# A four-layer graph network on one core: which source tiles of layer 3 are multiplied already during layer 2

## The chip, the core and the metric

The kernel runs on one core of one Trainium2 chip. The metric is the device time of one execution in microseconds, smaller being better; three runs of the kernel before have a median of 3042.52 us (3040.0 to 3048.64). A separate execution was profiled; the profile rows come from that one. The engines are named as in the profile: PE multiplies matrices (PEld is its weight load), DVE works on vectors, ACT on activations and copies, POOL issues the gathers, SP and the ACT queue issue the plain transfers.

## The reference

A graph has 6250 nodes with 256 features each and 100,000 edges, sorted by destination; destinations crowd at low node numbers (a uniform number squared). The features are layer-normed and clipped at zero, and four graph layers and a final product follow:

```python
h = sage_mean(h)   # h @ W1_self + mean over in-edges of h[src] @ W1_neigh + b1
h = sage_pool(h)   # h @ W2_self + max over in-edges of relu(h @ W2_pool + b)[src] @ W2_neigh + b2
h = sage_gcn(h)    # (sum over in-edges of h[src] + h) / (deg + 1) @ W3_neigh + b3
h = sage_mean(h)   # as layer 1, with W4
out = x + (h @ W_fc + b_fc)
```

The weights of layers 3, 4 and the last product are multiplied together ahead of time, so layer 3 sums rows of 512 numbers and layer 4 rows of 256.

## The kernel before

**Tiles.** Nodes stand in 49 tiles of 128 rows (`NT`), edges in 782 columns of 128 (`T`). A destination tile with a low number has very many edges. For those the kernel does not gather row by row: it makes a *count matrix* (how often does each source node appear among the edges of this destination), one 128 x 128 block for each pair of destination and source tile, and multiplies it with the source rows. `HUB = (8, 16, 18)` says for how many destination tiles that is done in layers 1, 3 and 4. In layer 3 these are the destinations 0 to 15, and each needs all 49 source tiles. The remaining destinations of a layer come out of `sums`: one indirect gather of 128 rows for each edge column, and three products with a one-hot matrix that add them up (rows are kept as three bf16 parts, hence three products).

**Layer 2** takes a maximum[...], so all 782 edge columns are gathered by POOL (`X<-tab_p,srcIf`, L1144), compared along runs of equal destinations by DVE (L1149), and written back by SP (`runb<-X`, L1190). The counter `at` numbers these columns: "step" below always means this counter. The columns are walked in six blocks from the last to the first, of 100, 130, 180, 220, 100 and 52 steps, so blocks end at steps 100, 230, 410, 630, 730 and 782. In the last three blocks two neighbouring columns are merged before they are written, which is one more DVE operation for every two steps (L1185). When a block is finished, a carry is passed between its 128 rows (`carry`), and then the destination tiles whose edges begin in it can be finished: `done2(d)` gathers the maxima (`tot`, L1053), transposes them, multiplies with the weights (`pm_prf`, L1077, L1080, L1083), and writes the row of tile `d` in three parts (`r`, L286 to L289) to `tab_r` (L1093). Tiles are finished from 48 down to 0; a new one is started about every 13 steps from step 112, or later where its block is not done.

**Work put beside the steps.** Behind each step a fixed portion of other work is written into the program:

- `hub.advance` makes the count matrices of destinations 8 to 15 until step `EARLY_AT` = 250, then those of 16 and 17 (destinations 0 to 7 were made in layer 1). They go to `tab_a`.
- `early.advance` does layer 3's products that are possible already. When four finished tiles (`BATCH`) of the range `EARLY` are there, `early_products` adds, for each of the 16 destinations, one load of four count blocks (`ae<-tab_a`, L1115, 64 KB, on SP's queue), 12 products (`pd<-r,ae`, L442), and one addition to the destination's sum (`acc`, `add3`: the first on ACT at L944, the others on DVE at L941). Below, these 12 products with their load and their addition are called a *parcel*; there are 8 x 16 = 128 of them. At each step a fortieth of what waits is done.

A row tile `r` stands in a ring of 9 buffers; it becomes free when the last product that reads it is done. The generators only write the program; a planner of the framework then sets the order on each engine, so the order in the built program need not be the order in which the generators ran.

**Layer 3** begins when `tab_r` is complete. The 17 source tiles outside `EARLY` are loaded as three resident pieces (`zt<-tab_r`, L1240), and the products of 16 destinations with them are spread over the gathered columns (`ring<-tab_r`, L386, and `pg`, L404). A gathered destination 16 to 48 also adds its own row: from the resident piece if it lies there (`d in Z3`), else by a load of 384 KB (`zown<-tab_r`, L1264) three steps ahead; `pm_own` (L1270) is the product that brings it in. The result goes to `tab_s`, and layer 4 begins after the last of it.

Of the kernel before, what the change touches and what calls it, by code (L numbers as in the profile page):

```python
# [10 lines left out]
BF16 = mybir.dt.bfloat16  # L11
# [9 lines left out]
P = 128  # L21
# [7 lines left out]
Z_SIGMA = 5.0  # L29
WIN = 8  # L30
HUB = (8, 16, 18)
EARLY = (6, 38)
MADE_AT = 64
FIRST_AT = 112
EARLY_AT = 250
# [43 lines left out]
def fast_path(  # L79
# [18 lines left out]
    FH = W1_self.shape[1]  # L98
    FO = W_fc.shape[1]
    NT = (N + P - 1) // P  # L100
# [37 lines left out]
    H1, H3, H4 = HUB  # L138
# [82 lines left out]
    at = 0  # L221
# [9 lines left out]
    def bank(pool, tag, name, shape=None, bufs=None):  # L231
        t = pool.tile([P, FH], F32, tag=tag, name=name, **({"bufs": bufs} if bufs else {}))
        if shape is None:
            return t
        n = math.prod(shape)
        if len(shape) == 1:
            return t[:, :n]
        return t[:, :n].rearrange("p (a b) -> p a b", b=shape[1])
# [566 lines left out]
    with ExitStack() as on:  # L805
# [10 lines left out]
        def done1(d, acc):  # L816
# [23 lines left out]
            for k in range(KI):  # L840
# [12 lines left out]
                        lambda acc, d=d: todo.append(done1(d, acc)), extra=1)  # L853
                  for d in range(H1)]
        work = list(builds[0])
# [90 lines left out]
    with tc.tile_pool(name="fl2c", bufs=1) as ck, ExitStack() as late:  # L946
# [102 lines left out]
        def totals(d):  # L1049
            tots = []  # L1050
            for b in range(b_of[d][0], b_of[d][1] + 1):
                t = wk.tile([P, FH], F32, name="tot", bufs=4)
                nc.gpsimd.indirect_dma_start(  # L1053
                    out=t, out_offset=None, in_=runs[b],
                    in_offset=bass.IndirectOffsetOnAxis(ap=rows_of[b][:, d : d + 1], axis=0),
                )
                tots.append(t)
            th = wk.tile([P, 2 * KI, P], F32, name="th2", bufs=2)
            nc.scalar.dma_start(th, tab_t[d].rearrange("p (k n) -> p k n", n=P))
            return tots, th  # L1060

        def done2(d):
            tots, th = totals(d)
            for _ in range(4):
                yield
            hm = tots[0]
            for t in tots[1:]:
                nc.vector.tensor_tensor(hm, hm, t, op=ALU.max)
            yield
            pt = bank(pst, "pt", "pt_hTf", (KH, P))  # L1070
            for j in range(KH):
                nc.tensor.transpose(pt[:, j, :], hm[:, j * P : (j + 1) * P], ident)
            hT = wk.tile([P, KH, P], F32, name="hTf")
            nc.scalar.copy(hT, pt)  # L1074
            pm = bank(psm, "pm", "pm_prf")
            for k in range(KI):
                nc.tensor.matmul(pm, th[:, k, :], usA[:, k, :], start=(k == 0), stop=False)  # L1077
            yield
            for k in range(KI):
                nc.tensor.matmul(pm, th[:, KI + k, :], usB[:, k, :], start=False, stop=False)  # L1080
            yield
            for c in range(KH):
                nc.tensor.matmul(pm, hT[:, c, :], un[:, c, :], start=False, stop=(c == KH - 1))  # L1083
                if c == 1:
                    yield
            pr = wk.tile([P, FH], F32, name="prf")
            nc.vector.tensor_add(pr, pm, prow)
            yield
            if d < H3:
                add3(d, pr)  # L1090
            r3 = early_pool[0].tile([P, 3 * FH], BF16, name="r3", bufs=2 * BATCH + 1)
            parts(pr, FH, r3)
            nc.sync.dma_start(tab_r[d * P : (d + 1) * P, :], r3)  # L1093
            if EARLY[0] <= d < EARLY[1]:
                ready.append((d, r3))
                if len(ready) == BATCH or d == EARLY[0]:
                    early_products()
            yield


        BATCH = 4
        ready = []
        early = Hub()
        early_pool = []

        def early_products():
            batch = dict(ready)
            ss = sorted(batch)
            ready.clear()
            for d in range(H3):  # L1110
                got = {}

                def load(d=d, got=got):
                    got[0] = early_pool[0].tile([P, BATCH, P], F8, name="ae", bufs=LOOK + 3)
                    nc.sync.dma_start(got[0][:, : len(ss), :].bitcast(BF16),  # L1115
                                      tab_a[d, :, ss[0] : ss[-1] + 1, :])

                work = dense(ss, lambda s, got=got: got[0][:, s - ss[0], :],
                             lambda s: batch[s], FH, psd, lambda v, d=d: add3(d, v))
                early.add([(load, work[0])] + work[1:])  # L1120


        todo = [chains(), node_rows(wk, psm)]
# [10 lines left out]
        at = 0  # L1134
        for b in reversed(range(NB)):
            tb = BLOCKS[b]
            t0 = offs[b] // P
            prev = None
            for s0 in range(0, tb, G2):
                n = min(G2, tb - s0)  # L1140
                X = (xmore if at // G2 % 2 else xpool).tile([P, G2, FH], F32, name="X2")
                for k in range(n):
                    t = t0 + s0 + k
                    nc.gpsimd.indirect_dma_start(  # L1144
                        out=X[:, k, :], out_offset=None, in_=tab_p,
                        in_offset=bass.IndirectOffsetOnAxis(ap=srcI[:, t : t + 1], axis=0),
                    )
                    if s0 + k:
                        nc.vector.scalar_tensor_tensor(  # L1149
                            X[:, k, :], prev, same[:, t : t + 1], X[:, k, :],  # L1150
                            op0=ALU.mult, op1=ALU.max,
                        )
                    prev = X[:, k, :]
                    at += 1
                    if at > 8:
                        next(steps, None)
                        if todo and next(todo[0], 0) == 0:
                            todo.pop(0)
                    if at == MADE_AT:
                        for _ in steps:  # L1160
                            pass
                        top.close()
                        early_pool.append(
                            top.enter_context(tc.tile_pool(name="early3", bufs=1)))
                    if at <= EARLY_AT:
                        hub.advance(math.ceil(len(first) * max(0, at - 16) / (EARLY_AT - 16)))
                    else:
                        hub.advance(len(first) + math.ceil(
                            len(rest) * (at - EARLY_AT) / (T - 100 - EARLY_AT)))
                    early.advance(early.done + math.ceil(early.left() / 40))  # L1170
                    if s0 + k > 2 and ends and next(ends[0], 0) == 0:
                        ends.pop(0)
                        tiles += [d for d in reversed(range(NT)) if b_of[d][0] == last_b]
                    if tiles and not ends and begun2 < NT * (at - FIRST_AT) / (T - 20 - FIRST_AT):
                        now.append(done2(tiles.pop(0)))
                        begun2 += 1
                    for g in list(now):
                        if next(g, 0) == 0:
                            now.remove(g)
                r0 = s0  # L1180
                if b < MERGED:
                    r0 = s0 // 2
                    if s0 + n < tb:
                        t = t0 + s0 + 1
                        nc.vector.scalar_tensor_tensor(  # L1185
                            X[:, 0, :], prev, same[:, t : t + 1], X[:, 0, :],
                            op0=ALU.mult, op1=ALU.max,
                        )
                        n = 1
                nc.sync.dma_start(  # L1190
                    runs[b][r0 * P : (r0 + n) * P, :].rearrange("(g p) f -> p g f", p=P),
                    X[:, :n, :],
                )
            end = carry(b, prev)
            next(end)
            ends.append(end)
            last_b = b
# [45 lines left out]
    with ExitStack() as on:  # L1243
# [8 lines left out]
        with tc.tile_pool(name="fl3", bufs=2) as wk:  # L1252
# [29 lines left out]
                    if d == s1 - 1:  # L1282
                        Z4.update(resident(zk, tab_s, FO, s0, s1))

            late = ((EARLY[1], 44), (44, NT), (0, EARLY[0]))
            Z3 = {}
            for s0, s1 in late:
                Z3.update(resident(wk, tab_r, FH, s0, s1))
# [2 lines left out]
            work = []  # L1291
            for d in range(H3):
                work += dense([s for s0, s1 in late for s in range(s0, s1)], lambda s, d=d: block(d, s), lambda s: Z3[s], FH, psd,
                              lambda acc, d=d: todo.append(done3(d, acc)))
# [3 lines left out]
        with tc.tile_pool(name="fl4", bufs=2) as wk:  # L1298
# [19 lines left out]
            work = []  # L1318
            for d in range(H4):
                work += dense([s for s0, s1 in order for s in range(s0, s1)],  # L1320
                              lambda s, d=d: block(d, s), lambda s: Z4[s], FO, psd,
                              lambda acc, d=d: todo.append(done4(d, acc)))
# [644 lines left out]
```

## Time and profile before

| what | value |
|---|---|
| median of three runs | 3042.52 us |
| the profiled execution: its time, its span | 3044.61 us, 3042.8 us |
| PE busy | 2459.1 us (81%) |
| DVE busy | 2039.5 us (67%) |
| POOL busy | 2051.3 us (67%) |
| mean granted PE clock | 0.909 |
| layer 2, first gather to last write of `tab_r` | about 824 to 2148 us |
| layer 3, from there to layer 4's first load | about 2148 to 2622 us |

The span is what lies between the first and the last instruction; 1.8 us of the execution lie around it. A busy share is an average over stages with different limits, so it says little by itself; what matters is which engine is full in which stage. "Releaser" or "waited for" names what ended an idle time.

### The profile page before, as it was taken

How to read it: one execution, taken by the hardware profiler on the slowest of the kernel's cores; microseconds unless marked ns; L12 is line 12 of the kernel's file. 1: busy time of each engine (PE TensorE's matmuls, PEld its weight loads, DVE VectorE, ACT ScalarE, POOL GpSimd, SP SyncE). 2: the span in 40 equal slices, each digit the busy share in tenths (PEclk: the TensorE clock that was granted, in tenths of full speed). 3: DMA queues.
4: the chain of work that ended last, by engine and by line, in shares of the span. 5: the costliest groups of instructions: out<-in, count | busy, mean ns of one | idle time of the engine just before them, and what ended most of it. 6: DMA issues, size and time to landing. Idle time of an engine off the chain costs nothing. (4 is left out here: it accounts for less than half of the span.)

```text
span 3042.8 us, 41553 instructions
## 1 busy us (share of the span) xinstructions
PE 2459.1 (81%) x12699; PEld 1402.3 (46%) x12699; DVE 2039.5 (67%) x5161; ACT 905.7 (30%) x2383; POOL 2051.3 (67%) x2260
## 2 busy tenths in 40 slices
PE   1468999999778664767789994983699999799999
PEld 0234666666543321323334442431234444488888
DVE  4956767766378788666779997987266676444433
ACT  2557766765255666421111110100000001000000
POOL 5274777776366676777767777765477777677775
PEclk9787999999999776788899997996799999899999
DMA  6454667776599999999989998987799999878886
GB/s 191 148 158 134 202 206 213 213 214 206 165 387 354 334 390 376 363 387 387 371 275 318 323 315 280 310 287 223 291 368 385 383 381 375 310 234 239 247 239 193
DMA packets 380021, 865.41 MB, mean 284 GB/s; under 512 B 58078, under 2 KB 151238, under 8 KB 379756
## 3 DMA queue, kind: packets, MB, share of 16 engines
q0 software_dynamic: 146560, 514.74, 51.8%
q1 hardware_dynamic: 175144, 292.49, 25.9%
q10 hardware_dynamic: 58084, 55.44, 5.8%
q8 instruction: 103, 1.69, 0.2%
q14 instruction: 130, 1.06, 0.1%
HBM read 610.65 MB, written 252.60 MB: 284 GB/s over the span
## 5 line engine op out<-in xcount | busy, mean ns | idle before, releaser
L1144 POOL DMA_INDIRECT X<-tab_p,srcIf x782 | 839.8, 1074 | 384.5 <-issue 161.5
L404 PE MATMUL pg<-ring,hot 128*128 128x256 bf16 (+2 forms) x3390 | 682.6, 310 | 78.3 <-DMA ring<-tab_h,srcT 34.8
L442 PE MATMUL pd<-zt,ac 128*128 128x256 bf16 (+1 forms) x3462 | 566.8, 299 | 21.6 <-DMA ac<-tab_a 12.2
L386 POOL DMA_INDIRECT ring<-tab_h,srcT x474 | 451.5, 952 | 195.8 <-PE pg L404 76.9
L404 PEld LDWEIGHTS <-hot 128*128 128x128 bf16 x3390 | 332.7, 99 | 303.1 <-issue 134.9
L442 PE MATMUL pd<-r,ae 128*128 128x512 bf16 x1536 | 378.5, 396 | 96.5 <-DVE acc L941 45.2
L386 POOL DMA_INDIRECT ring<-tab_r,srcE x342 | 330.6, 967 | 146.5 <-PE pg L404 63.6
L442 PEld LDWEIGHTS <-ac 128*128 128x128 fp8e4 x3462 | 339.4, 98 | 151.7 <-issue 21.0
L311 ACT ACTIVATE hs<-ht,onef 128x128 bf16<-128x128 bf16 x781 | 292.3, 395 | 305.3 <-PE pb L319 303.6
L319 PE MATMUL pb<-hm,hs 128*128 128x392 bf16 x781 | 257.4, 380 | 152.4 <-ACT A L324 109.4
L386 POOL DMA_INDIRECT ring<-tab_s,srcE x314 | 298.7, 951 | 112.8 <-issue 60.5
L423 DVE SCALAR_TENSOR_TENSOR acc<-pg,M,acc 128x257 f32<-128x257 f32 (+2 forms) x518 | 273.0, 561 | 151.4 <-PE pg L404 150.6
L1149 DVE SCALAR_TENSOR_TENSOR X<-X,samef 128x512 f32<-128x512 f32 x391 | 292.0, 748 | 97.6 <-DMA X<-tab_p,srcIf 84.0
L1149 DVE SCALAR_TENSOR_TENSOR X<-X,samef,X 128x512 f32<-128x512 f32 x385 | 287.2, 747 | 92.9 <-DMA X<-tab_p,srcIf 46.1
L442 PEld LDWEIGHTS <-ae 128*128 128x128 fp8e4 x1536 | 155.1, 101 | 330.4 <-issue 153.2
L382 DVE TENSOR_SCALAR hot<-iota_bf,keyE 128x128 bf16<-128x128 bf16 x656 | 153.5, 268 | 132.2 <-PE pg L404 126.0
L1083 PE MATMUL pm_prf<-unf,hTf 128*128 128x512 f32 x392 | 199.6, 637 | 2.8 <-ACT hTf L1074 2.8
L319 PEld LDWEIGHTS <-hs 128*128 128x128 bf16 x781 | 81.9, 105 | 249.5 <-issue 165.3
L442 PE MATMUL pd<-Z,A 128*128 128x256 bf16 (+1 forms) x1176 | 189.1, 274 | 0.3 <-ACT A L324 0.2
L313 DVE TENSOR_SCALAR hm<-iota_w,mk 128x392 bf16<-128x392 f16 x461 | 154.5, 344 | 46.0 <-PE pb L319 44.8
L324 ACT ACTIVATE A<-pb 128x392 fp8e4<-128x392 f32 x288 | 139.3, 486 | 147.7 <-DVE most L323 113.8
L323 DVE TENSOR_REDUCE most<-pb 128x1 f32<-128x392 f32 x288 | 160.8, 559 | 32.6 <-PE pb L319 31.9
(288 smaller groups left out, 2881.9 us busy)
## 6 DMA issues: line engine op xcount, KB each, us to landing
runb<-X SPq DMA_DIRECT2D x208, 512.0 KB
runb<-X SPq DMA_DIRECT2D x183, 256.0 KB
tab_r<-r SPq DMA_DIRECT2D x49, 384.0 KB
tab_a<-A SPq DMA_DIRECT2D x18, 784.0 KB
tab_t<-th SPq DMA_DIRECT2D x49, 256.0 KB
tab_p<-hpf SPq DMA_DIRECT2D x49, 256.0 KB
th<-tab_t ACTq DMA_DIRECT2D x49, 256.0 KB
X<-tab_p,srcIf POOLq DMA_INDIRECT x782
```

The lines of the kernel that those rows point to most:

```text
L311: nc.scalar.activation(hots[0], t, AF.Relu, bias=one, scale=-1.0)
L313: nc.vector.tensor_scalar(hots[1], iota_w, mk[:, r : r + 1], None, op0=ALU.is_equal)
L319: nc.tensor.matmul(hold[0], hots[0], hots[1], start=(k == 0), stop=(k == k_of[w] - 1))
L323: nc.vector.tensor_reduce(most[:, w : w + 1], hold[0], AX.X, ALU.max)
L382: nc.vector.tensor_scalar(hot[j], iota_b, keyT[:, j - jb : j - jb + 1], None, op0=ALU.is_equal)
L386: nc.gpsimd.indirect_dma_start(out=ring[:, j % deep, : 3 * F], out_offset=None, in_=table, in_offset=bass.IndirectOffsetOnAxis(ap=srcT[:, ...
L404: nc.tensor.matmul(pg[:, : F + c], hot[j], X[:, part * F : (part + 1) * F + c], start=(k == 0 and part == 2), stop=(k == n - 1 and part == 1),
L423: nc.vector.scalar_tensor_tensor(acc[d], pg, m, acc[d], op0=ALU.mult, op1=ALU.add)
L442: nc.tensor.matmul(hold[0][:, : F + c], a, z[:, part * F : (part + 1) * F + c], start=(s == ss[0] and part == 2), stop=(s == ss[-1] and pa ...
L1083: nc.tensor.matmul(pm, hT[:, c, :], un[:, c, :], start=False, stop=(c == KH - 1))
L1144: nc.gpsimd.indirect_dma_start(out=X[:, k, :], out_offset=None, in_=tab_p, in_offset=bass.IndirectOffsetOnAxis(ap=srcI[:, t : t + 1], axis=0),
L1149: nc.vector.scalar_tensor_tensor(X[:, k, :], prev, same[:, t : t + 1], X[:, k, :], op0=ALU.mult, op1=ALU.max,)
```

## The change

`EARLY` becomes 17 to 48: layer 2 multiplies the tiles that are finished first, and the residents of layer 3 are the tiles 0 to 16 that are finished last. The first two batches are then ready before the count matrices of destinations 8 to 15 exist; their parcels are collected in `later` and added at step 257. The ring of row tiles grows from 9 to 16. In `done2`, eight steps instead of four lie between the gather of the maxima and their use.

```diff
-EARLY = (6, 38)
+EARLY = (17, 49)
@@ done2
             tots, th = totals(d)
-            for _ in range(4):
+            for _ in range(8):
                 yield
@@
-            r3 = early_pool[0].tile([P, 3 * FH], BF16, name="r3", bufs=2 * BATCH + 1)
+            r3 = early_pool[0].tile([P, 3 * FH], BF16, name="r3", bufs=4 * BATCH)
@@
         early = Hub()
+        later = []
@@ early_products
-                early.add([(load, work[0])] + work[1:])
+
+                put = later.extend if H1 <= d and at <= EARLY_AT + 6 else early.add
+                put([(load, work[0])] + work[1:])
@@ the loop over steps
+                    if at == EARLY_AT + 7:
+                        early.add(later)
                     early.advance(early.done + math.ceil(early.left() / 40))
@@ layer 3
-            late = ((EARLY[1], 44), (44, NT), (0, EARLY[0]))
+            late = ((0, 7), (7, 14), (14, EARLY[0]))
```

## The prediction, made before the changed kernel ran

> **What bounds the kernel now.** I read the page's slices first, to see which engine is full where.
>
> ```profile
> PE   1468999999778664767789994983699999799999
> DVE  4956767766378788666779997987266676444433
> POOL 5274777776366676777767777765477777677775
> PEclk9787999999999776788899997996799999899999
> DMA  6454667776599999999989998987799999878886
> ```
>
> A slice is 76 us. From the 12th on layer 2 is full in its transfers (DMA 9); around the 22nd DVE and PE are full instead; the last third is PE's. I then cut layers 2 and 3 at the times when POOL issued the gathers of steps 160, 250, 440, 640 and 782, and asked for busy times per stretch: us, then PE, PEld, DVE, ACT, POOL with counts, granted PE clock, DMA share, GB/s.
>
> ```profile
> 1097.00:1245.00 148.00, 85.87 (x217) 36.28 (x216) 126.50 (x276) 97.58 (x276) 99.50 (x95) 0.70 1.02 379
> 1245.00:1514.00 269.00, 192.41 (x607) 83.75 (x605) 167.19 (x265) 51.65 (x110) 196.09 (x184) 0.83 1.02 380
> 1555.00:1867.00 312.00, 270.30 (x1042) 122.88 (x1042) 291.93 (x470) 52.53 (x114) 231.94 (x213) 0.95 0.94 310
> 1867.00:2112.00 245.00, 182.53 (x613) 81.17 (x611) 201.17 (x308) 19.93 (x33) 171.22 (x160) 0.86 0.88 284
> 2192.00:2490.00 298.00, 285.06 (x1285) 124.74 (x1285) 199.84 (x481) 25.08 (x62) 218.41 (x225) 0.99 1.00 378
> 2490.00:2616.00 126.00, 122.88 (x564) 54.83 (x562) 87.09 (x206) 12.94 (x32) 86.62 (x91) 1.00 0.95 355
> ```
>
> Until step 420 (1514 us) the transfers bound, at 380 GB/s, and PE and DVE have room. In steps 440 to 640 DVE is busy 94% and PE 87%: there an addition costs its time. In steps 640 to 782 nothing is quite full. What it is made of is in the groups of that stretch (count, busy us, mean ns, idle before and its releasers):
>
> ```profile
> L442 PE MATMUL pd<-r,ae 128*128 128x512 bf16 x384 | 94.0, 396 | 14.3 <-DVE acc L941 14.3
> L1077 PE MATMUL pm_prf<-usA,th 128*128 128x512 f32 x43 | 23.7, 673 | 2.5 <-DVE fixf L1040 2.2 <-DVE prf L1087 0.3
> L941 DVE TENSOR_TENSOR acc<-acc,pd 128x512 f32<-128x512 f32 x32 | 21.8, 680 | 1.3 <-PE pd L442 1.3
> L1144 POOL DMA_INDIRECT X<-tab_p,srcIf x142 | 152.3, 1072 | 67.6 <-issue 31.8 <-DVE X L1149 17.9 <-DVE X L1185 7.6
> ```
>
> 384 products are 32 parcels: a parcel is 94.0/32 = 2.94 us of PE and 0.68 us of DVE here. POOL waits 17.9 + 7.6 = 25.5 us for DVE to free the gather tiles; the rest of its time is its own issuing.
>
> **The change, stage by stage.** The order of the two built programs gives the counts. I counted parcels (by their additions, with the 16 first ones on ACT) and finished tiles between the layer-2 operations of DVE. By steps 160-250, 250-420, 420-440, 440-640, 640-782: parcels 0, 31, 8, 57, 32 before and 16, 42, 9, 61, 0 after; tiles 6, 12, 1, 14, 12 before and 6, 9, 2, 17, 12 after (one more tile slips out of the steps before 160). So 16 parcels move into the first stage and 11 into the second, six go in between, and 32 leave the last; and four tiles fall behind because parcels stand before them on PE.
>
> *Steps 160-250.* 16 loads of 64 KB are 1.05 MB, at 379 GB/s 2.8 us, in full since the transfers bound. PE gets 16 x 2.94 = 47 us on 86 of 148, DVE 8 x 0.68 = 5.4 on 126.5, ACT 8 copies: room for all, but PE is in order and the count-matrix products stand behind the parcels. The loads go through SP's queue, in front of the writes that free gather tiles. At least 2.8; at most 10 (the DVE and ACT time in full on top). I take +3, near the transfer row.
>
> *Steps 250-420.* 11 more parcels: 0.72 MB, +1.9 us. Four tiles fewer before step 420: each reads a maximum (256 KB) and a factor (256 KB) and writes a row (384 KB), 0.92 MB, so three in this stage are -2.75 MB, -7.2 us. PE: 192.4 + 11 x 2.94 - 3 x 9.0 = 198 of 269 us (9.0 us: the four groups of tile products of the last stretch, 99.3 us over 11 tiles). By bytes -5; but 18 parcels and four tiles crowd into steps 250-310, 53 + 36 = 89 us of PE in 96. I take -2, between -5 and +12.
>
> *Steps 420-640.* 5 parcels and 4 tiles more. DVE: 5 x 0.68 + 4 x 3 x 0.685 = 11.6 us. In full it is +12; if DVE's idle 20 us of 312 take it, 0. I take half, +6. PE's side is the first rival.
>
> *Steps 640-782.* No parcels are left: -94 us PE, -21.8 us DVE. POOL's own floor is 142 gathers x (1.07 + 0.30 issue) + 14 maxima x 1.39 = 214 us, and what can go is its wait for DVE, 25.5 us; I take -24, ends -45 (gathers also shorter) and 0. A first rule of the Trainium skill bears on the far end: *SBUF — State Buffer*, "Who interferes with whom", says that DVE and GpSimd share one port pair under an exclusive lock, that a DVE operation with two SBUF inputs contends with a GpSimd instruction that reads SBUF, and that one with a single SBUF input does not. The gather takes 1.07 us here and 0.95 in layer 4, so something of the kind is seen. If the parcels' additions caused it, their removal would bring 142 x 0.12 = 17 us more; but they read one operand from PSUM, while the comparisons that stay read two tiles. By the rule I leave the 17 us out: -24, not -41.
>
> *The two other edits of layer 2.* The ring of 16 takes memory only; ACT once waited 12.7 us for a row buffer behind PE, in the last stretch, and DVE's next row step behind it; that is within the 24. Eight steps instead of four: DVE waits 28.5 us in all, six times, for gathered maxima, with comparisons queued behind. In the built order the first maximum stands two comparisons later, at the other block ends the distance to its gather is unchanged: 0, at best -3. Behind a held-back parcel nothing waits.
>
> *Layer 3.* PE bounds it: 285 of 298 us. The start is a transfer:
>
> ```profile
> 2145.51 2.27 DMA tab_r<-r
> 2148.99 43.38 DMA zt<-tab_r
> ...
> PE pd L442 <- DMA zt<-tab_r: 4.3, 1, 4.3
> ...
> zown<-tab_r SPq DMA_DIRECT2D x20, 384.0 KB
> ```
>
> The chain runs through the third resident piece, and PE waits 4.3 us for it. The pieces are 7, 7, 3 tiles instead of 6, 5, 6, the same 17; the third is first read three gathered columns later in PE's order (by `pm_own` of tile 16), so the 4.3 us go. Against that, tiles 38 to 48 are no longer resident: 11 more `zown` loads (one, tile 16, fewer at the start), 11 x 393 KB = 4.33 MB, in the last 126 us. There the rate is 355 GB/s; layer 3's first 43 us moved 391, so (391 - 355) x 126 us = 4.5 MB are free: +0 to +3, I take 2.5. Here a rule speaks against the change: the same page's "A bandwidth-pool intuition that's wrong" gives about 358 GB/s between HBM and a core; with that nothing is free and 4.33 MB cost 12.1 us. The trace moves 391, so the row decides: by it the whole sum is -16, by the rule -6. Last, tile 48's own load now lies at the end, before layer 4 may begin; nearest is the row write above, 2.27 us for the same 384 KB: +2.5. Layer 3: -4.3 + 2.5 + 2.5 = +1.
>
> **Sum:** 3 - 2 + 6 - 24 + 1 = -16 us. On the span, 3042.8 - 16 = 3026.8; the runs' median is 0.3 below that span, so 3026.5.
>
> **Rivals.** *PE becomes the bound in steps 420-640 (slower).* Four tiles x 9.0 + 5 parcels x 2.94 = 51 us more PE in 353 us, of which PE is idle only 52; PE and DVE wait for each other in order, and the reserve is used up. It decides once the stage grows by more than 25 us; I put +40 there, and -24 in the last stage becomes -14 because nine tiles stand behind each other (9 x 9.0 = 81 us of PE in steps 648-683). Sum 3 - 2 + 40 - 14 + 1 = +28: 3070. For it speaks PE's 87% and the four late tiles; against it that its busy time is modelled and a product issues about every 0.22 us in layer 3 (1.29 us for 6), where 2.94/12 = 0.245 stands here. *The last stage does not get faster (no change).* Before, steps 620-640 and 760-780 have no parcels and took 31.8 and 35.4 us, 1.68 a step, against 245/142 = 1.73 on average: then the gain is 142 x 0.05 = 7, the sum +1: 3043. Against it: 6.7 us in the first and about 7 in the second are waits at block ends. *Layer 3 takes the gain back:* `zown` in full, 12, and 6 at the end: sum -1: 3041.
>
> **Numbers.** The forecast has 0.50, the PE rival 0.29, the unchanged last stage 0.13, layer 3 0.08. A change of 0.3%, 9 us, is about what a measurement of this kernel can tell from none. Faster 0.50, same 0.21, slower 0.29. The forecast's own range adds its bounds: 3008 to 3034. For 8 in 10 I go to 3002 (the far end of the last stage) and up to 3068, which leaves out the upper half of the PE rival.
>
> **What would show it.** Right: no `pd<-r,ae` in the last 140 gathers of layer 2, that stretch near 221 us, POOL's wait for DVE gone from it; steps 440-640 about 6 us longer; 32 `zown` loads, none waited for, and no 4.3 us at `zt`. Wrong: PE at 95% in steps 250-640 with DVE waiting for `pd` or `pm_prf`, the last stretch at 235 or more, PE waiting for `ring<-tab_r` late in layer 3.

## The result, and the profile after

| | before | after |
|---|---|---|
| median, runs side by side | 3043.07 us (3040.0 to 3048.64, 4 runs) | 3064.49 us (3053.04 to 3068.04, 4 runs) |
| ratio, 95% interval | | 1.007 [1.0049, 1.009] |
| profiled execution: its time, its span | 3044.61, 3042.8 us | 3053.04, 3051.2 us |

The change makes the kernel slower by 21 us. The profiled execution of the changed kernel was the fastest of its four, so this profile shows 8 us of the 21; a later profile of the same kernel (called the second profile below, span 3063.0 us) shows 20, and both are used. Two executions of one kernel can differ by several microseconds in a stage (steps 250 to 420: 263.8 and 271.4 us in these two), so a difference of that size in a single profile is not told from none. First the slices of the changed kernel, in the same layout as those shown of before:

```profile
PE   1468999999778577777788998812599999799999
DVE  4956766766378788666688998877266666444444
POOL 5274777776366666677756776775477777577775
PEclk9777999999998788998899999955899999899999
DMA  6454667776599999999988998987799999888886
```

In slices 25 to 28, the end of layer 2, PE's row has 8 8 1 2 where it had 4 9 8 3: the parcels are gone from there. In exchange there is a dent in the middle: in slices 21 and 22, POOL has 5 and 6 (before 6 and 7), and the transfers 8 and 8 (8 and 9). The stretches with their busy times say it in microseconds. The five are steps 160-250, 250-420, 440-640, 640-782, and layer 3:

```profile
1094.00:1242.00 148.00, 114.80 (x401) 50.87 (x407) 127.67 (x278) 99.31 (x281) 94.79 (x92) 0.88 1.02 378
1242.00:1506.00 264.00, 186.19 (x654) 80.76 (x666) 171.24 (x267) 37.36 (x79) 193.37 (x186) 0.86 1.03 384
1542.00:1882.00 340.00, 304.41 (x1125) 138.78 (x1145) 304.20 (x486) 61.91 (x133) 237.89 (x216) 0.96 0.89 291
1882.00:2120.00 238.00, 103.31 (x254) 47.20 (x252) 188.77 (x299) 26.32 (x48) 171.21 (x159) 0.70 0.89 290
2152.00:2635.00 483.00, 431.11 (x1902) 188.52 (x1941) 302.90 (x737) 39.65 (x98) 333.99 (x343) 0.98 0.98 371
```

Steps 440 to 640 took 312 us before and take 340, at 291 GB/s instead of 310. DVE's work in it grew by 12 us, PE's by 34 and the stretch by 28; both engines are now busy 89.5% (DVE 94% and PE 87% before). The last stage lost 79 us of PE and became only 7 us shorter. Its gathers' row and its first tile product:

```profile
L1147 POOL DMA_INDIRECT X<-tab_p,srcIf x141 | 152.9, 1084 | 55.0 <-issue 29.3 <-DVE X L1190 9.2 <-DVE X L1152 5.4
L1077 PE MATMUL pm_prf<-usA,th 128*128 128x512 f32 x44 | 24.5, 681 | 4.8 <-DVE fixf L1040 4.8
```

No `pd<-r,ae` is left there. POOL's wait for DVE fell from 25.5 us to 9.2 + 5.4 = 14.6; it did not go.

Where the time of all the kernels lies, from their profiles, is this table. The stages are cut at POOL's gathers of the steps named; "maxima" is the place in the planned order, counted in DVE's comparisons, of the first maximum that needs two blocks, at the end of the third block (step 410). A span is that of the profiled execution, a ratio that of all its runs to those of the kernel before on the same chip. Thin parcels have a third of their products.

| kernel | maxima | 160-250 | 250-420 | 420-500 | 500-640 | 640-782 | layer 3 | ratio |
|---|---|---|---|---|---|---|---|---|
| before | 428 | 143.1 | 273.4 | 139.3 | 213.7 | 244.7 | 477.2 | 1 |
| after | 472 | 147.5 | 263.8 | 156.3 | 220.3 | 238.0 | 482.4 | 1.007 |
| after, second profile | 472 | 144.7 | 271.4 | 153.5 | 222.9 | 233.8 | 484.6 | 1.0063 |
| parcels spread, after_pace160 | 435 | 141.3 | 272.0 | 140.3 | 214.6 | 231.8 | 484.8 | 0.9987 |
| eight steps alone | 429 | 140.0 | 276.8 | 128.6 | 216.8 | 236.3 | 477.8 | 0.9953 |
| before, last 32 parcels out | 428 | 142.4 | 272.8 | 138.8 | 213.0 | 226.4 | 476.0 | 0.9962 |
| after, first 32 parcels out | 447 | 140.6 | 267.7 | 146.0 | 218.2 | 231.3 | 483.4 | 1.0038 |
| before, thin parcels | 418 | 147.4 | 280.8 | 141.5 | 207.5 | 237.8 | 481.3 | 0.9995 |
| after, thin parcels | 419 | 145.7 | 275.2 | 137.8 | 203.7 | 231.7 | 481.3 | 0.998 |

On chips of one kind (the kernel before at 3039 to 3043 us), and with all products in each parcel, steps 420 to 640 get longer as these maxima come later: 353.0 us at place 428, 354.9 at 435, 364.2 at 447, 376.6 and 376.4 at 472. The eight steps alone (429) lie below this row, with 345.4.

Most of the growth lies in steps 420 to 500 (14 to 17 us), the 80 steps after the end of the third block. Steps 420 to 500 and 500 to 640 of the kernel before, then of the changed kernel:

```profile
1514.00:1653.00 139.00, 122.71 (x455) 55.01 (x455) 119.46 (x197) 23.39 (x52) 99.20 (x92) 0.95 0.91 295
1653.00:1867.00 214.00, 178.69 (x696) 81.93 (x694) 201.68 (x331) 37.55 (x82) 160.18 (x146) 0.94 0.94 311
```

```profile
1506.00:1662.00 156.00, 127.97 (x453) 57.67 (x461) 122.52 (x200) 24.09 (x52) 96.18 (x91) 0.92 0.81 257
1662.00:1882.00 220.00, 209.35 (x791) 96.11 (x804) 209.91 (x331) 43.35 (x93) 165.27 (x148) 1.00 0.94 313
```

In steps 420 to 500 DVE does 3 us more and PE 5, in 17 us more: the loss there is waiting. Steps 500 to 640 are another matter. DVE does 8 us more in a stretch that is 7 to 9 us longer; it is busy 95% of it, as PE is, and none of its waits there is for PE. So this part of the growth reads as the additional work of DVE.

What happens in the first part is seen in DVE's own timeline of the changed kernel (start, duration, line, operation, and in brackets the idle time before it):

```profile
1616.98 0.68 DVE L287 TENSOR_TENSOR prf<-prf,r 128x512 f32<-128x512 f32 x1
1617.58 0.68 DVE L941 TENSOR_TENSOR acc<-acc,pd 128x512 f32<-128x512 f32 x1
1625.33 0.74 DVE L1068 TENSOR_TENSOR tot<-tot 128x512 f32<-128x512 f32 x1 [7.07 <-DMA tot<-runb,rows_of]
1625.99 0.68 DVE L289 TENSOR_TENSOR r<-prf,r 128x512 bf16<-128x512 f32 x1
...
1627.49 0.67 DVE L941 TENSOR_TENSOR acc<-acc,pd 128x512 f32<-128x512 f32 x1
...
1635.53 0.69 DVE L1068 TENSOR_TENSOR tot<-tot 128x512 f32<-128x512 f32 x1 [5.81 <-DMA tot<-runb,rows_of]
1636.14 0.68 DVE L941 TENSOR_TENSOR acc<-acc,pd 128x512 f32<-128x512 f32 x1
```

DVE stands twice at a gathered maximum, and behind it, in its queue, stand the last part of a row (`r`, L289), which the next parcel's products need, and a parcel's addition (L941), which frees PE's accumulator. So PE stands too, and POOL. The waits of steps 440 to 500 of the changed kernel (total, times, longest):

```profile
DVE tot L1068 <- DMA tot<-runb,rows_of: 12.9, 2, 7.1
POOL X L1147 <- DVE X L1152: 11.6, 5, 4.9
PE pd L442 <- DVE r L289: 10.8, 2, 6.2
PE pd L442 <- DVE acc L941: 9.8, 3, 7.0
POOL X L1147 <- DVE X L1190: 8.2, 6, 4.9
...
POOL tot L1053 <- DVE tot L1068: 6.0, 1, 6.0
...
PE pd L442 <- DMA ae<-tab_a: 3.5, 1, 3.5
```

In the kernel before, the same event comes around step 440, with waits of 6.2 and 3.5 us, and PE waits only 2.0 us for a row part in all of steps 420 to 500. In the changed kernel it comes some 40 steps later, because the tiles of the third block are finished late, and there it meets a row that a parcel is waiting for.

### The profile page after: what moved, and what is told of

Read it like the earlier page. It is cut to its first block, busy times and chain, and to the rows that moved or that the text cites. A ratio compares the mean times of both kernels' runs of the same rounds, so it can differ in the third digit from the quotient of the medians.

```text
span 3051.2 us, 41459 instructions
## 1 busy us (share of the span) xinstructions
PE 2428.8 (80%) x12616; PEld 1393.6 (46%) x12699; DVE 2047.1 (67%) x5161; ACT 905.7 (30%) x2383; POOL 2044.7 (67%) x2260
## 5 line engine op out<-in xcount | busy, mean ns | idle before, releaser
L1147 POOL DMA_INDIRECT X<-tab_p,srcIf x782 | 831.0, 1063 | 397.5 <-issue 158.0
L442 PE MATMUL pd<-r,ae 128*128 128x512 bf16 x1492 | 387.0, 402 | 115.5 <-DVE acc L941 74.0
L423 DVE SCALAR_TENSOR_TENSOR acc<-pg,M,acc 128x257 f32<-128x257 f32 (+2 forms) x518 | 272.8, 560 | 169.2 <-PE pg L404 168.7
L1083 PE MATMUL pm_prf<-unf,hTf 128*128 128x512 f32 x392 | 191.1, 616 | 3.9 <-ACT hTf L1074 3.8
L309 ACT ACTIVATE ht<-iota_bf,sk 128x128 bf16<-128x128 bf16 x461 | 172.0, 396 | 7.0 <-DVE bad L767 0.5
```

What stands on the lines that cost most here:

```text
L309: nc.scalar.activation(t, iota_b, AF.Abs, bias=sk[:, r : r + 1])
L423: nc.vector.scalar_tensor_tensor(acc[d], pg, m, acc[d], op0=ALU.mult, op1=ALU.add)
L442: nc.tensor.matmul(hold[0][:, : F + c], a, z[:, part * F : (part + 1) * F + c], start=(s == ss[0] and part == 2), stop=(s == ss[-1] and pa ...
L1147: nc.gpsimd.indirect_dma_start(out=X[:, k, :], out_offset=None, in_=tab_p, in_offset=bass.IndirectOffsetOnAxis(ap=srcI[:, t : t + 1], axis=0),
```

## The experiments

All took place on five chips, each group of runs on one. On the first two chips the kernel before has medians of 3502 and 3447 us, on the other three 3039 to 3040; ratios are always to the kernel before on the same chip.

### The changed kernel on another chip, and its small edits by themselves

**The changed kernel again** (no edit).

> The changed kernel once more, unchanged, for a second profile and more times (they spread from 3053 to 3068 us, and the profile on record is the fastest of them). Theory A, the backlog: parcels put in front make four tiles late, and steps 420-640 are where it is paid; then the time is again 10 to 25 us above the kernel before, and steps 420-640 again take 20 us or more over its 353 us. If a slower execution has its extra 10 us in that stage too, the stage is also what varies; if the extra lies in layers 3 and 4, something else varies.

Measured: 0.9998 [0.997, 1.0026]. On this chip the change costs nothing that the runs can tell. Steps 420 to 640 are 396.7 us there, against 379.7 and 383.0 in the two variants of the kernel before below; the last stage is 244.0 against 255.7 and 254.8.

**Eight steps undone in the changed kernel.**

```diff
-            for _ in range(8):
+            for _ in range(4):
```

> The changed kernel with four steps instead of eight between the gather of the maxima and their use. Theory B, the eight steps: a tile stays longer in its buffers, two tiles overlap, and the later maxima hold DVE where it is full; then this gives most of the loss back: within 5 us of the kernel before, steps 420-640 near 355 us. Theory A: no more than 5 us of difference to the changed kernel, steps 420-640 still over 370 us.

Measured: 1.001 [0.9988, 1.0031], steps 420 to 640 393.9 us. Undoing the eight steps gives nothing back that the runs can tell, so they are not what makes these steps long.

**The two small edits without the move.**

```diff
-            for _ in range(4):
+            for _ in range(8):
@@
-            r3 = ... bufs=2 * BATCH + 1)
+            r3 = ... bufs=4 * BATCH)
```

> The kernel before with the two small edits alone, ring of 16 rows and eight steps. Theory A: no change, within 4 us of before, since nothing moves. Theory B: slower by 10 to 20 us.

Measured: 0.9962 [0.9942, 0.9982], faster by 15 us on this chip. So the move of the parcels costs more than the whole change shows: 0.9998 against 0.9962. But where the parcels are moved, the gain is not found: there four and eight steps are alike (1.001 and 0.9998).

**Layer 3's additional loads without the move.** The tiles that are not destinations of the count matrices take their own row by a load although it is resident.

```diff
-                    if d in Z3:
+                    if d in Z3 and d < H3:
```

> The kernel before, except that in layer 3 the tiles 38 to 48 load their own row once more instead of taking it from the resident pieces, as in the changed kernel: 11 loads of 384 KB more at the end of layer 3, everything else as before. My prediction: +5 us (2.5 for the transfers, 2.5 for the last tile's load). The rival that layer 3 takes it back: +12 to +18 us, with PE waiting for gathered rows. If the reads are hidden altogether: 0.

Measured: 0.9999 [0.9976, 1.0022]; in the profile layer 3 takes 534.9 us against 530.3 in the kernel with the small edits. About 5 us as one reads it from the profiles, not told from nothing by the runs.

**Which of the small edits** was settled on two other chips, each edit alone.

> The kernel before with eight steps instead of four between the gather of the maxima and their use, and nothing else. Together with the ring of 16 rows this made the kernel before 0.38% faster. If the eight steps do it: 0.996 of the kernel before here. If the ring does it: 1.000, within 0.2%.

> The kernel before with a ring of 16 row tiles instead of 9, nothing else. Eight steps alone gave 0.9953, both edits together 0.9962 on another chip. If the eight steps are all of it: 1.000, within 0.2%. If the ring has a part: 0.997 or less.

Measured: the eight steps 0.9953 [0.9939, 0.9966], the ring 0.9998 [0.9987, 1.001]. The ring is worth nothing, the eight steps 14 us. Before, DVE stood 6.2 and 3.5 us at the maxima around step 440; with eight steps it stands once:

```profile
1544.30 0.69 DVE L1068 TENSOR_TENSOR tot<-tot 128x512 f32<-128x512 f32 x1 [5.59 <-DMA tot<-runb,rows_of]
1553.08 0.69 DVE L1068 TENSOR_TENSOR tot<-tot 128x512 f32<-128x512 f32 x1
```

Steps 420 to 500 fall from 139.3 to 128.6 us. In these steps DVE's own wait for maxima fell only from 9.7 to 5.6 us (in all of layer 2 from 28.5 to 25.8), while POOL's wait for DVE's comparisons fell from 12.2 to 4.6: less than half of the 10.7 us is that wait itself, and the rest fits what no longer queues behind it. This kernel, with one number changed, beats both.

### What freeing the last stage is worth

**The last 32 parcels of the kernel before left out**, on two chips.

```diff
-EARLY = (6, 38)
+EARLY = (14, 38)
@@ layer 3
-            late = ((EARLY[1], 44), (44, NT), (0, EARLY[0]))
+            late = ((EARLY[1], 44), (44, NT), (0, 6))
```

> The kernel before, with layer 3's products inside layer 2 for the tiles 14 to 37 only: the 32 parcels of the tiles 6 to 13, which run in the last 140 gathers, are left out, and with them that part of layer 3's sum (and four loads of 64 KB for each tile less). This measures by itself what freeing the last stage is worth. The forecast's step (the last stage is held up by its parcels): steps 640 to 782 about 24 us shorter than in the kernel before, the whole about 20 to 30 us shorter, 0.992 of its time. The rival that the last stage does not get faster (gathers bound it): about 7 us there, the whole 5 to 12 us shorter, 0.997. Under both, steps 420 to 640 stay within 3 us.

> The kernel before with the source tiles 14 to 37 inside layer 2: the last 32 parcels (tiles 6 to 13) and their part of layer 3's sum are left out, so that the last 140 gathers have none. The forecast's step: steps 640 to 782 about 24 us shorter, 0.992. The rival (gathers at their own pace and two block ends make this stage): about 7 us, 0.997.

Measured: 0.9966 [0.9943, 0.9989] and 0.9962 [0.9946, 0.9977], that is 12 us, half of what the forecast took and more than the 7 of its rival. The last stage in the second profile, and its gathers:

```profile
1866.00:2092.00 226.00, 92.58 (x230) 41.91 (x228) 182.59 (x276) 19.44 (x33) 174.92 (x159) 0.71 0.91 299
```

```profile
L1144 POOL DMA_INDIRECT X<-tab_p,srcIf x141 | 156.1, 1107 | 45.5 <-issue 30.5 <-DVE X L1149 5.9 <-DMA runb<-X 4.3
```

POOL's wait for DVE is nearly gone here (5.9 us). The stage is 226.4 us, against 238.7 in the kernel with the ring alone on the same chip and 244.7 in the profile of before. 20 steps without a tile or a parcel take 28 to 30 us, whatever else was taken out: 142 steps at 1.43 are 203 us, and the rest is the two block ends.

### Which parcels cost the time

**The first 32 parcels of the changed kernel left out**, on two chips.

```diff
-EARLY = (17, 49)
+EARLY = (17, 41)
```

> The changed kernel with the source tiles 17 to 40 inside layer 2: the first 32 parcels, those of the tiles 41 to 48, are left out, and with them that part of layer 3's sum. Backlog (the parcels that come before step 420 push tiles back, and the late tiles cost the time in steps 420 to 640): the late tiles are gone, steps 420 to 640 fall by about 20 us to the length that they have in the kernel before or below it, the whole is 25 to 40 us shorter than the kernel before (0.989). If instead the five additional parcels and the tight block end at steps 460 to 500 cost it, without regard to what came earlier: steps 420 to 640 keep 15 us or more of the difference, the whole is within 10 us of the kernel before.

> The changed kernel with the source tiles 17 to 40 inside layer 2: the first 32 parcels (tiles 41 to 48) and their part of layer 3's sum are left out. If the backlog that they make on PE before step 420 is what the loss consists of: steps 440 to 500 fall from about 120 us to under 105, steps 420 to 640 to 350 or less, the whole to 0.992 of the kernel before. If what counts is the work inside steps 420 to 640: these stay at 362 us or more, the whole is within 0.3% of the kernel before or above it.

Measured: 0.9972 [0.9953, 0.9992] on the first chip, 1.0038 [1.0025, 1.005] on the second, with steps 420 to 640 at 384.4 and 364.2 us; what the backlog branches expect (0.989 and 0.992) was missed on both. On the second chip the amount of work does not explain the loss: with 32 parcels less (94 us of PE at the forecast's 2.94 each) the kernel is still slower than the kernel before, and 0.76% slower than the kernel before with 32 parcels out, which has as many parcels (96) and none in the last stage either. It shares with the changed kernel that the maxima come late (447, not 428; 12 us more in steps 420 to 640 than its counterpart) and that layer 3 is long (7 us more).

**The change by half.**

```diff
-EARLY = (17, 49)
+EARLY = (12, 44)
@@ layer 3
-            late = ((0, 7), (7, 14), (14, EARLY[0]))
+            late = ((44, NT), (0, 6), (6, 12))
```

> The change by half: the source tiles 12 to 43 inside layer 2 (resident pieces 44-48, 0-5, 6-11). Backlog: about half of the loss in steps 420 to 640 (8 to 12 us over the kernel before) and, as about 16 parcels stay in the last stage, 3 to 6 us gained there; the whole lies within 8 us of the kernel with the two small edits alone. If the loss comes with the first tiles that are finished early alone (17 to 48 against 6 to 37 makes the parcels start with the very first tiles), none of the loss remains and the whole is 5 us or more faster than the small edits alone.

Measured: 1.0001 [0.9977, 1.0026]; steps 420 to 640 388.0 us with 67 additions of parcels in steps 440 to 640, the maxima at 465. On this chip nothing told it from the kernel before; the comparison with the small edits alone, which the expectation speaks of, is missing on it.

**The parcels spread over twice as many steps.**

```diff
-                    early.advance(early.done + math.ceil(early.left() / 40))
+                    early.advance(early.done + math.ceil(early.left() / 80))
```

> The changed kernel with the parcels spread over twice as many steps: at each step an eightieth of the parcels' work that is left is issued, not a fortieth. Backlog: fewer parcels stand in front of the tiles in steps 160 to 420, so steps 420 to 640 get shorter by 8 us or more against the changed kernel and parcels come back into the last stage, which gets longer by up to 10; the whole within 10 us of it, rather faster. If PE is simply full in steps 420 to 640 with the work that falls there, whatever the order: 420 to 640 gets longer still, as parcels of the front move into it, and the whole is 5 to 15 us slower than the changed kernel.

Measured: 1.0001 [0.9976, 1.0026] on the same chip, steps 420 to 640 379.2 us, the maxima at 454. By the time this decides nothing.

### Is PE what carries it

**A third of the products in each parcel**, in both kernels, with loads and additions as they were.

```diff
-            for part in (2, 0, 1):
+            for part in parts:
@@ (the default of `parts` and the start and stop marks, which follow it, are left out here)
@@ early_products
-                             lambda s: batch[s], FH, psd, lambda v, d=d: add3(d, v))
+                             lambda s: batch[s], FH, psd, lambda v, d=d: add3(d, v),
+                             parts=(0,))
```

> The kernel before, in which each parcel multiplies only one of the three parts of the row tiles: 4 products instead of 12, with the same loads and the same additions; two thirds of these products are left out (1024 of them, about 250 us of PE). If PE holds layer 2 up (the rival of the prediction in its place, steps 420 to 640): these steps get 15 us or more shorter, steps 640 to 782 about 10 shorter. If gathers, comparisons and block ends bound it and PE does not: both stay within 5 us of the kernel before, the whole within 0.3%.

> The changed kernel with the same cut: 4 products in a parcel instead of 12, loads and additions unchanged, two thirds of the parcels' products left out. If PE is what the change loses to in steps 420 to 640: against the same cut of the kernel before those steps are less than 8 us longer (DVE's share of five more parcels and four tiles), the maxima that straddle the end of the third block come back to about step 430, and the whole is 10 us or more faster than the cut kernel before. If DVE and the waits at the block end cost it, with PE only standing behind them: those steps stay 14 us or more longer than in the cut kernel before, and the whole is within 5 us of it.

Measured: 0.9995 [0.9984, 1.0005] and 0.998 [0.9968, 0.9991]. Taking 214 us of PE out of the kernel before gains nothing that the runs can tell. In the changed kernel it takes the whole loss away; it is then 4 us faster than its counterpart, less than the 10 us that the first branch expects. Steps 420 to 640, first of the cut kernel before, then of the cut changed kernel:

```profile
1526.00:1875.00 349.00, 165.42 (x495) 73.48 (x494) 298.02 (x474) 39.48 (x81) 265.26 (x236) 0.72 0.91 298
```

```profile
1522.00:1864.00 342.00, 160.69 (x508) 72.39 (x507) 300.61 (x475) 40.00 (x79) 263.75 (x237) 0.74 0.92 304
```

The difference of 23.6 us has become -7.5, and the planned order, which reckons with PE's load, has the maxima back at 419. So PE's load makes the loss; whether by the order or by standing in the way at run time, this pair does not tell.

**Six buffers for the gathered maxima** instead of four.

```diff
-                t = wk.tile([P, FH], F32, name="tot", bufs=4)
+                t = wk.tile([P, FH], F32, name="tot", bufs=6)
```

> The changed kernel with six buffers for gathered maxima instead of four. In the changed kernel's trace POOL waits 6 us at the end of the third block for DVE to free such a buffer, and the gathers of the edges queue behind it. If that wait is a link of the stall in steps 460 to 500: steps 420 to 640 are 5 to 8 us shorter than in the changed kernel. If it only mirrors DVE's lateness: within 3 us, POOL waiting for DVE's comparisons instead.

Measured: 1.0049 [1.0032, 1.0066], steps 420 to 640 369.6 us, 7 us less than in the two profiles of the changed kernel, as the first branch expects. The runs lie between the changed kernel's and no change; its own ratio was 1.007 and 1.0063 on other chips, and the intervals overlap. At most a small link.

### The order alone

Thin parcels change both the load and the order. The last pair changes little but the order: all products, parcels and loads are there, six parcels fewer come before step 420 (52 instead of 58), and nine come in the last stage.

```diff
-                    early.advance(early.done + math.ceil(early.left() / 40))
+                    early.advance(early.done + math.ceil(early.left() / 160))
```

> The changed kernel with the parcels handed over more slowly: at each step a 160th of what is left, not a fortieth. By the planned order, 36 parcels' additions (42 in the changed kernel) still come before step 420 and 59 (61) in steps 440 to 640, 9 (0) in the last stage; but the tiles are no longer late: 12 (9) in steps 250 to 420, 14 (17) in 440 to 640, the straddling maxima after comparison 435 (472). If the late tiles are what the loss consists of: steps 420 to 640 are 353 us or less (376.6 and 369.6 with the change as it is), the whole is not slower than the kernel before, 0.997 to 1.001. If it is the parcels themselves, wherever the tiles are, or layer 3's loads: 365 us or more there, the whole 1.004 or more.

> The changed kernel itself, for comparison on this chip. If this chip is like the first one: 1.004 to 1.009 of the kernel before, steps 420 to 640 at 368 us or more. If it is like the one with the long layer 1: 1.000.

Measured: 0.9987 [0.9976, 0.9998] with the parcels spread, 1.0063 [1.004, 1.0086] for the changed kernel on the same chip; medians 3035.26 and 3057.77 us. With the tiles back in their places 22 us are gone, all of the loss; steps 420 to 640 take 354.9 us, 2 more than the first branch expects. Steps 420 to 500 of the kernel with the parcels spread, to be laid beside the 156 us of the changed kernel above:

```profile
1514.00:1654.00 140.00, 122.55 (x447) 56.31 (x456) 122.55 (x205) 28.20 (x61) 99.90 (x92) 0.95 0.91 297
```

In the changed kernel DVE did the same 122.5 us of work, POOL 4 us less and PE 5 us more, in 16 us more. So it is waiting, not work. The waits of the kernel with the parcels spread, in its steps 440 to 500:

```profile
DVE tot L1068 <- DMA tot<-runb,rows_of: 11.2, 2, 7.7
PE pd L442 <- DVE acc L941: 10.9, 5, 7.0
POOL X L1147 <- DVE X L1190: 6.6, 5, 3.1
...
POOL X L1147 <- DVE X L1152: 2.4, 7, 0.6
```

DVE waits for the maxima as long as in the changed kernel (11.2 and 12.9 us). But no row part stands behind it (`PE pd <- DVE r`, 10.8 us, is gone), and POOL waits 9 us for DVE's comparisons instead of 19.8, and hardly at all for a buffer of maxima (6.0 us in the changed kernel). That the order costs the time is shown by this pair; that it does so by this meeting of a maximum and a row part is read from the waits, and no run takes the two apart.

### Parcels added to the last stage

What follows from the last stage's 12 us was tried on the fastest kernel: 16 more parcels there, to relieve layer 3.

```diff
-EARLY = (6, 38)
+EARLY = (2, 38)
@@ done2
-            for _ in range(4):
+            for _ in range(8):
```

> The kernel before with eight steps between gather and use, and the source tiles 2 to 37 instead of 6 to 37 inside layer 2 (residents 38-43, 44-48, 0-1): 16 more parcels, all in the last 140 gathers. If parcels there are hidden behind gathers and block ends: steps 640 to 782 grow by less than 8 us against the eight steps alone, layer 3 loses 16 x 12 products (about 40 us of PE at 0.22 us each, of which its transfers, 98% busy, let through a part: 10 to 25 us), the whole 0.990 of the kernel before. If the last stage is as full as the forecast took it (0.75 us for a parcel): 12 us or more are given back there, the whole not faster than the eight steps alone (0.995).

Measured: 0.9949 [0.9933, 0.9966], not told from the eight steps alone (0.9953). The last stage grew by 2 us and the tail after it by 3, as the first branch expects. But layer 3 gained nothing of the 10 to 25 us. Its window with eight steps alone, then with 16 parcels fewer in it:

```profile
2130.00:2607.00 477.00, 433.59 (x1941) 189.41 (x1941) 303.26 (x734) 39.64 (x98) 329.27 (x342) 0.97 0.98 367
```

```profile
2139.00:2616.00 477.00, 407.12 (x1749) 170.48 (x1749) 300.37 (x735) 39.65 (x98) 333.75 (x342) 0.96 0.97 362
```

26.5 us of PE are gone and the stage is as long as it was. Both have their transfers 97 to 98% busy, which fits a stage that the transfers bound; no run here shows it.

## Why the prediction was wrong, by its own steps

The forecast said -16 us; the change costs 21. Of the 37 us between them, some 18 lie in steps 420 to 640, 13 to 17 in the last stage and 4 to 6 in layer 3. The forecast named the way in which it would be wrong, the rival that PE becomes the bound in steps 420 to 640. That rival's place and sign are right, its mechanism in part; its sum, +28, comes near only because it erred in both directions: it has +40 for the stage, where 23.5 were measured, and -14 for the last stage, where 7 to 11 were gained.

- **Steps 420 to 640, +6: this step failed.** Measured +23.6 and +23.4 in the two profiles. Its amount of work was right: DVE's busy time grew by 11.3 us, 11.6 were forecast. Wrong was that idle time would take half of it: DVE's idle time grew too, by 12 us. In steps 500 to 640 the additional work cost its full time. In steps 420 to 500 waiting came on top, a term that the step had at nothing: the late tiles stood in it as work, but their lateness cost more. Spreading the parcels puts the tiles back and the stage is at 354.9 us, 2 us over the kernel before, with all parcels but nine still ahead of the last stage.
- **The rival's mechanism.** It had PE full throughout and no reserve left. In steps 500 to 640, where the stage grew by 7 to 9 us, PE is 95% busy, but so is DVE, and DVE does not wait for PE there. In steps 420 to 500, with 14 to 17 us of the loss, PE is only 82% busy: the planned order let PE's load push the tiles back, and the time is then lost to waits between DVE, PE and POOL. Of the signs named for it, the long last stretch came (238.0 and 233.8 us); DVE waited for `pd` only 3.6 us in steps 420 to 640 (2.1 before), and in the last 130 us of layer 3 PE waited 2.3 us for `ring` (1.4 before).
- **Steps 640 to 782, -24: mis-sized.** Measured -6.7 and -10.9. By itself the removal of these parcels is worth 12 us (the two runs with 32 parcels out). The length without parcels was reckoned right to within 6 us (221; 226.4 measured), but in the change its two block ends take longer (79.1 us for steps 640 to 680 and 39.0 for 740 to 760, against 74.0 and 33.8 where the parcels are left out of the kernel before), 14.6 us of POOL's wait for DVE remain, and the profile of before shows the stage longer (244.7) than the kernel with the ring alone does (238.7). The 17 us for shorter gathers were rightly left out by the rule of the Trainium skill (*SBUF — State Buffer*, "Who interferes with whom"): without the parcels' additions the gathers did not become shorter (1.107 us, 1.072 before). The trace agrees with the rule directly. In steps 160 to 782 of the kernel before, 557 gathers ran beside a comparison of DVE, which reads two tiles, and took 1.092 us on average; the 37 with DVE idle and the five beside nothing but a parcel's addition took 0.946.
- **The two small edits at 0, "at best -3": wrong** for the eight steps. Alone they gain 14 us; the waits that the step counted (28.5 us) fell by less than 3, and the rest of the gain fits what they had held up. In the changed kernel this gain was not found: on the first chip the runs with four and with eight steps are alike. The ring at 0 was right.
- **Steps 160 to 250, +3, and 250 to 420, -2: not contradicted**, at +4.4 and +1.6, and -9.6 and -2.0. The -9.6 lies outside the stated -5 to +12, but the two profiles of the one kernel differ by nearly 8 us in this stage, so these figures do not prove the step either.
- **Layer 3, +1: the sum was low by 4 to 6 us.** Measured +5.2 and +7.4. The wait for the third resident piece did not go: PE still waits for `zt`, 3.4 us of 4.3. The last tile's own load, put at 2.5, is the larger part: from layer 3's last gather to layer 4's first the kernel takes 20.0 and 20.7 us instead of 16.4, and 18.8 instead of 14.6 where the loads were tried without the move. That leaves 2 to 4 us for the bytes of the additional loads, near the 2.5 taken from the trace and far from the 12.1, an estimate from the 358 GB/s of the Trainium skill (*SBUF — State Buffer*, "A bandwidth-pool intuition that's wrong"); the whole stage moves 371 GB/s, more than that figure, so here the measured rate decides. PE's waits in the stage name no `zown` load, as forecast. The step's "PE bounds it" does not hold: 26.5 us of PE less did not shorten the stage.
- **Two sums do not come out.** The third rival's terms (-4.3, 12 and 6 in layer 3) give -3 in all, not -1, and the bounds of the steps add up to about 2990 to 3078 us, not 3008 to 3034. Neither is why the forecast failed.

In the sum: against the kernel with the eight steps alone, which lies 14 us below the kernel before, the move costs about 35 us (1.007 against 0.9953). 22 are the order in which tiles and parcels stand. For the rest, some 13, the profiles of the two kernels (parcels spread, and eight steps alone) show 7 us more in layer 3 and 12 more in steps 420 to 500, where the gain of the eight steps is missing, and a few less elsewhere; no run takes it apart.

## What to carry to other kernels

When work is moved ahead of a chain that other engines wait for, price the delay of the chain, not only the work: here moving the products cost 21 us, and moving nearly all of them in another order nothing, depending on whether the planned order let them push the tiles past a block end. Before moving work into a "free" stage or out of a "full" one, measure by leaving it out what it is worth where it stands; 94 us of PE in the last stage were worth 12, and 214 in all of layer 2 nothing. And take an engine's idle time off a cost only where it is known what that idle time waits for. A short in-order wait also costs what stands behind it: four more steps between a gather and its use gained 14 us, nearly what the whole move had promised.

## What the runs showed of the hardware

Chips differ. On two of the five, layer 1 takes 1040 to 1076 us instead of 823 to 827, and PE's granted clock there is 0.83 to 0.86 instead of 0.93 to 0.94; the kernel before is 13 to 15% slower on them. On the one of them where it was run, the change makes no difference (0.9998); it costs 0.6 to 0.7% elsewhere; in the same way the changed kernel without its first 32 parcels has 0.9972 on one of the two and 1.0038 on another chip. Why the loss is not seen on these two stays open: in the profiles, steps 420 to 640 get longer and steps 640 to 782 shorter on both kinds of chip.
